# Regrouping the routing of a mixture-of-experts layer: groups of 3, 4, 4, 4 and 1 batches

## The chip, the cores and the metric

The kernel runs on one core of a Trainium2 chip. The metric is the device time of one execution in microseconds, as the median of several runs. The engines are named as in the profile: PE multiplies matrices, PEld is its weight load, DVE, ACT and POOL are the vector, scalar and general engines, and SP issues most DMAs.

## The reference

Two decoder layers with layer norms ahead of each part: self-attention, cross-attention over a context of 375 rows and a mixture of experts, twice. There are 16 batches of 112 tokens, 256 wide. The change concerns the seam between the second layer's cross-attention and its mixture of experts. The router of that mixture is this, cut to what matters:

```python
logits = x @ router_w + router_b                     # 8 experts
top, ei = top_k(logits, 2); probs = softmax(top)
# per batch: first choices of all tokens, then second choices, are counted up per expert
pos = cumsum(one_hot(ei), axis=0) * one_hot - 1       # place of the token in its expert's buffer
# 33 places per expert and batch; tokens past these are dropped
buf[ei, pos] += x
h = buf @ w_c_fc + b_c_fc;  g = buf @ w_gate + b_gate
o = silu(h * g) @ w_c_proj + b_c_proj
out = x + sum_k probs[k] * o[ei[k], pos[k]]
```

## The kernel before

The work is tiled by batch: the 112 tokens of one batch lie on partitions. The second cross-attention is one loop over 32 steps `(b, u)`, batch and half of the heads. A step turns the softmaxed scores of this step on PE (L1493), issues the scores of the next one (L1461, row maxima L1472, Exp L1473, division on POOL L1484), takes one item from a list called `after`, and then makes keys and values of the next batch, the projection of the batch before (L1315 adds it to `x_res`), the queries, and the values (L1509). The keys and values of batches 4, 8 and 12 (and 0) were made earlier in the program and are loaded, so the steps of batches 3, 7 and 11 have less PE work; batch 15 has no successor.

PE's order in this section is the order of the program (`manual_schedule` for PE). DVE, ACT, POOL and SP are put in order by the compiler's scheduler, and each then runs its list strictly in that order. In the section that follows, the feed-forward part, DVE and PE both follow the program.

The list `after` carries the routing. `routed(b)` makes a batch's logits (`logits1`, L1219 adds the bias). With the fourth batch of a group, `route1` finds the two best experts of the four batches on the DVE (`top_two`, L297 to L305) and makes the two softmax shares (`prob`, L1227 to L1231). It returns `places`, which takes the counting products with a triangle of ones on PE (here called P) and from these, on the DVE, each token's position, expert, slot number `place`, and the number `need` of tokens per expert past the first 12 (L1247 to L1264). After it come four `dispatch1`: `slot_rows` builds a 0/1 row of 264 slots for each token (L1285, L1286) and normalises x again (L238), PE multiplies the two (L1275, the slot products), and DVE (first half) and ACT (second half) copy the result into `first_in` and `more_in` (L1278, L1279). The last group, batches 12 to 15, is not in the list: it is routed and dispatched at the head of the feed-forward section.

There, `ranks` orders the experts by `need` (L1660 to L1681) and gives the numbers by which weights for the fullest experts are fetched; SP waits for them ahead of the third weight unit. Then come 12 units: two experts by number and one by rank, four times. `hidden(n, j)` makes one of eight products of a unit, with ACT (L1766) and DVE (L1767) behind it, and each `hidden` is followed by one item of the list `jobs` (bias rows by rank, and the matrices of softmax shares by which results are added up).

Some names more: `mv1` and `r1` are mean and reciprocal deviation of each token (POOL makes the latter, L242 and L243), `xn15` is the normalised batch 15, kept in its own place because the last projection writes it there.

Of the kernel before, what the change touches and what calls it, by code (L numbers as in the profile page):

```python
# [9 lines left out]
F32 = mybir.dt.float32  # L10
U32 = mybir.dt.uint32
AF = mybir.ActivationFunctionType
# [17 lines left out]
P0 = 12  # L30
# [8 lines left out]
def _constants():  # L39
# [31 lines left out]
        "slots": rows(np.arange(E1 * CAP)),  # L71
# [27 lines left out]
def tile_decoder(ctx: ExitStack, tc: tile.TileContext, t: dict, out: bass.AP):  # L99
# [137 lines left out]
    def normed(dst, src, mv, r):  # L237
        nc.vector.tensor_scalar(dst, src, mv, r, ALU.subtract, ALU.mult)  # L238
# [6 lines left out]
    def norm_one(lp, b, keep=None, affine=None, dst=None):  # L245
# [10 lines left out]
        normed(xn, x[:, b, :], mv[:, 0:1], r)  # L256
# [30 lines left out]
    def top_two(lp, v, n, rev):  # L287

        nb = v.shape[1]
        bn = lambda name: lp.tile([L, nb, n], F32, tag=f"tt_{name}", name=name, bufs=1)  # L290
        b1 = lambda name: lp.tile([L, nb], F32, tag=f"tt_{name}", name=name, bufs=1)
# [929 lines left out]
    def route1(lp, q):  # L1221

        bs = slice(4 * q, 4 * q + 4)
        (oh0, v0), (oh1, v1) = top_two(lp, lg1[:, bs, :], E1, const("rev8", L))

        p0, ex = prob[0][:, bs], prob[1][:, bs]
        nc.vector.tensor_sub(ex, v1, v0)  # L1227
        nc.scalar.activation(ex, ex, AF.Exp)
        nc.vector.tensor_scalar(p0, ex, 1.0, None, ALU.add)
        nc.vector.reciprocal(p0, p0)  # L1230
        nc.vector.tensor_mul(ex, ex, p0)  # L1231

        oh = [o.rearrange("p b n -> p (b n)") for o in (oh0, oh1)]

        def places():
            pc = bank()
            before = const("before", L)
            mm_sum(pc[:L, : 4 * E1], [(before, oh[0])])
            mm_sum(pc[:L, 4 * E1 : 8 * E1], [(before, oh[1]), (ones[:L, :L], oh[0])])
            b1 = lambda name: lp.tile([L, 4], F32, tag=f"rt_{name}", name=name, bufs=1)  # L1240
            tmp = lp.tile([L, 4, E1], F32, tag="rt_tmp", name="tmp", bufs=1)
            sums = lp.tile([L, E1], F32, tag="rt_sums", name="sums", bufs=1)
            for k in range(2):
                pos, ok, more = b1(f"pos{k}"), b1(f"ok{k}"), b1(f"more{k}")
                o3 = (oh0, oh1)[k]
                kept, ei = pos1[k][:, bs], exp1[k][:, bs]
                nc.vector.tensor_tensor(  # L1247
                    tmp, o3, pc[:L, 4 * k * E1 : 4 * (k + 1) * E1].rearrange("p (b n) -> p b n", n=E1), ALU.mult
                )
                nc.vector.tensor_reduce(pos, tmp, AX.X, ALU.add)  # L1250
                nc.vector.tensor_tensor(tmp, o3, over(const("io8", L), 4), ALU.mult)
                nc.vector.tensor_reduce(ei, tmp, AX.X, ALU.add)
                nc.vector.tensor_scalar(ok, pos, CAP - 0.5, None, ALU.is_lt)

                nc.vector.tensor_scalar(kept, pos, float(CAP - 1), None, ALU.min)

                nc.vector.scalar_tensor_tensor(pos, ei, float(CAP), kept, ALU.mult, ALU.add)
                nc.vector.scalar_tensor_tensor(pos, pos, 1.0, ok, ALU.add, ALU.mult)
                nc.vector.tensor_scalar(place[k][:, bs], pos, -1.0, None, ALU.add)

                nc.vector.tensor_scalar(more, kept, P0 - 0.5, None, ALU.is_gt)
                nc.vector.tensor_tensor(tmp, o3, bcast(more, E1), ALU.mult)
                nc.vector.tensor_reduce(sums, tmp.rearrange("p b n -> p n b"), AX.X, ALU.add)
                nc.vector.tensor_add(need, need, sums)  # L1264

        return places

    def dispatch1(lp, b, made=None):
# [4 lines left out]
        for c in range(2):  # L1273
# [3 lines left out]
            copy = nc.scalar.copy if c else nc.vector.tensor_copy  # L1277
# [3 lines left out]
    def slot_rows(lp, b):  # L1281
        slots = const("slots", L)
# [4 lines left out]
        xn = lp.tile([L, D], F32, tag="xn", name="xn", bufs=2)  # L1287
        normed(xn, x[:, b, :], mv1[:, b, 0:1], r1[:, b : b + 1])
# [8 lines left out]
    with ExitStack() as ph:  # L1297
# [243 lines left out]
        with tc.manual_schedule(engines={mybir.EngineType.PE}):  # L1541
# [46 lines left out]
            after = []  # L1588

            def routed(b):  # L1590
                logits1(b)
                if b % 4 == 3:
                    q = b // 4
                    places = route1(rp, q)
                    after.append(places)
                    if q < B // 4 - 1:
                        after.extend(lambda b=b: dispatch1(lp, b) for b in range(4 * q, 4 * q + 4))
# [38 lines left out]
        after.append(lambda: routed(B - 1))  # L1636
        while len(after) > 1:
            after.pop(0)()
# [7 lines left out]
    with ExitStack() as ph:  # L1646
# [180 lines left out]
        with tc.manual_schedule(engines={mybir.EngineType.DVE, mybir.EngineType.PE}):  # L1827
            late.pop(0)()
            while after:
                after.pop(0)()  # L1830
            made = {b: slot_rows(lp, b) for b in (B - 4, B - 3)}
            ranked = ranks()
            for b in range(B - 4, B):
                dispatch1(lp, b, made.pop(b))
                if b + 2 < B:
                    made[b + 2] = slot_rows(lp, b + 2)
            jobs = bias_of(0)
            jobs += share_jobs(share_first, KA, first_idx)
# [69 lines left out]
```

## Time and profile before

| | |
|---|---|
| Runs (us) | 1610.70, 1608.06, 1604.71 |
| Median (us) | 1608.06 |
| Profiled execution (us) | 1611.35 |
| Its span (us) | 1609.6 |
| Mean granted PE clock | 0.973 |
| DMA moved | 116.52 MB |

The profile is of one execution. Times within it count from the start of its span. The cross-attention loop of the second layer runs from about 954 to 1316 us, the feed-forward section from then to the end. "Idle before, releaser" beside an instruction is how long its engine stood and what ended it. The loop is told by its step number n = 2b + u; the step begins with its transposes (L1493).

### The profile page before, as it was taken

The page shows a single profiled execution, that of the slowest core. Times are in us where ns is not written, and L with a number is a line of the kernel's source. Part 1 is how long each engine was busy: PE and PEld are TensorE (multiplying, and loading weights), DVE is VectorE, ACT ScalarE, POOL GpSimd, SP SyncE. Part 2 cuts the span into 40 slices and gives each one's busy share as a digit, 9 for nine tenths or more (in the row PEclk, how much of TensorE's full clock was granted, in tenths as well). Part 3 has the DMA queues.
Part 4 walks back from the last instruction along what each step waited for, and adds up shares of the span by engine and source line. Part 5 has one row for each costly group of instructions (what it writes and reads, how often), then busy time and mean ns, then how long its engine had stood idle before and what let it go on. Part 6 is the DMA issues. An engine that isn't in the chain of part 4 may idle for free.

```text
span 1609.6 us, 30346 instructions
## 1 busy us (share of the span) xinstructions
PE 1501.8 (93%) x11438; PEld 1127.5 (70%) x11438; DVE 964.1 (60%) x2649; ACT 577.9 (36%) x1437; POOL 483.1 (30%) x647
## 2 busy tenths in 40 slices
PE   7898999999988896899999989999999978999998
PEld 5776777777754585778888756666666657788786
DVE  6986777777762353976677655566575566342124
ACT  3441444444442252223333233343434323333332
POOL 5642122222115352323333344544445420000000
PEclk9999999999999897999999999999999988999999
DMA  6500322222224476200000010101010012344421
GB/s 170 143 10 21 94 67 65 67 65 65 64 76 158 130 231 214 54 24 1 1 1 2 20 56 10 49 20 48 19 30 30 1 53 79 137 178 157 147 89 48
DMA packets 84929, 116.52 MB, mean 72 GB/s; under 512 B 13433, under 2 KB 70946, under 8 KB 84778
## 3 DMA queue, kind: packets, MB, share of 16 engines
q1 hardware_dynamic: 78690, 98.25, 20.1%
q0 software_dynamic: 3312, 8.54, 1.6%
q10 hardware_dynamic: 2776, 7.72, 1.4%
q8 instruction: 95, 1.56, 0.4%
q14 instruction: 56, 0.46, 0.1%
HBM read 84.41 MB, written 22.08 MB: 66 GB/s over the span
## 4 chain that ended last, share of the span: by engine, by line
PE 76%; DVE 13%; POOL 4%; DMA 3%; issue 2%; another core or an unknown queue 1%; ACT 1%; SPq 0%; POOLq 0%; DVEq 0%; ACTq 0%
PE pT L120 49%; PE pT L785 3%; PE pT L1461 3%; PE pT L1493 2%; POOL pr L1484 2%; DVE mx L769 2%; PE pT L1509 2%; PE pT L803 2%; PE pT L767 2%; PE pT L1358 2%; PE pT L1393 2%; PE pT L1379 2%; PE pT L620 1%; DVE st L234 1%
## 5 line engine op out<-in xcount | busy, mean ns | idle before, releaser
L1484 POOL TENSOR_SCALAR pr<-pr,den 112x375 f32<-112x375 f32 x128 | 157.0, 1244 | 176.9 <-DVE den L1482 157.7
L120 PE MATMUL pT<-xnT,w_all 128*128 128x224 f32 (+2 forms) x800 | 165.3, 358 | 0.6 <-DVE xnT L269 0.5
L120 PEld LDWEIGHTS pT<-xnT,w_all 128*128 128x128 f32 x800 | 145.9, 197 | 10.2 <-issue 5.7
L794 ACT ACTIVATE pr<-pT 125x336 f32<-125x336 f32 x256 | 94.6, 456 | 126.3 <-PE pT L785 126.3
L769 DVE TENSOR_REDUCE mx<-pT 112x1 f32<-112x375 f32 x256 | 122.2, 539 | 11.3 <-PE pT L767 9.9
L1371 POOL TENSOR_TENSOR pr<-pr,den 112x448 f32<-112x448 f32 x64 | 59.9, 956 | 198.8 <-DVE den L1369 147.9
L120 PE MATMUL pT<-w_all 128*128 (+3 forms) x376 | 113.1, 453 | 1.7 <-ACT w_all L392 0.8
L120 PE MATMUL pT<-w_all,cT 128*125 128x256 f32 (+1 forms) x336 | 111.4, 475 | 0.0
L120 PE MATMUL pT<-cT,w_all 128*128 128x375 f32 x320 | 110.2, 486 | 0.0
L120 PE MATMUL pT<-w_all,xnT 128*112 128x256 f32 (+1 forms) x320 | 105.7, 477 | 1.9 <-ACT xnT L566 0.9
L120 PE MATMUL pT<-w_all,oT 128*112 128x256 f32 x448 | 106.4, 383 | 0.6 <-DVE oT L1400 0.6
L242 POOL TENSOR_SCALAR nr<-nmv 112x1 f32<-112x1 f32 x96 | 22.3, 232 | 273.7 <-DVE nmv L235 273.1
L1308 ACT COPY pT<-pT 112x448 f32<-112x448 f32 (+1 forms) x64 | 34.0, 532 | 170.9 <-PE pT L1493 88.3
L120 PEld LDWEIGHTS pT<-w_all 128*128 128x128 f32 (+2 forms) x376 | 70.2, 190 | 33.8 <-issue 4.6
L1473 ACT ACTIVATE pr<-pT,top 112x375 f32<-112x375 f32 x128 | 72.4, 572 | 56.8 <-DVE top L1472 54.4
L120 PEld LDWEIGHTS pT<-cT,w_all 128*128 128x128 f32 x320 | 59.3, 190 | 41.1 <-issue 5.8
L120 PEld LDWEIGHTS pT<-w_all,oT 128*112 128x112 f32 x448 | 75.7, 177 | 16.3 <-DVE oT L1400 1.0
L120 PE MATMUL pT<-first_in,w_all 128*128 128x192 f32 x512 | 86.6, 329 | 0.0
L120 PEld LDWEIGHTS pT<-first_in,w_all 128*128 128x128 f32 x512 | 84.4, 192 | 1.5 <-issue 0.3
L120 PEld LDWEIGHTS pT<-w_all,cT 128*125 128x125 f32 x336 | 61.1, 187 | 33.3 <-issue 22.7
L120 PEld LDWEIGHTS pT<-w_all,xnT 128*112 128x112 f32 x320 | 57.1, 183 | 35.8 <-issue 22.4
L1767 DVE SCALAR_TENSOR_TENSOR hT<-pT,vT,gt 128x192 f32<-128x192 f32 x64 | 26.7, 417 | 90.5 <-ACT gt L1766 90.4
(306 smaller groups left out, 3019.2 us busy)
## 6 DMA issues: line engine op xcount, KB each, us to landing
w_all<-in_L_ffn_w_c_fc_dram SPq DMA_DIRECT2D x12, 1024.0 KB
w_all<-in_L_ffn_w_gate_dram SPq DMA_DIRECT2D x12, 1024.0 KB
w_all<-in_L_ffn_w_c_proj_dram SPq DMA_DIRECT2D x12, 1024.0 KB
cx<-in_ctx_dram SPq DMA_DIRECT2D x32, 375.0 KB
kz<-kn SPq DMA_DIRECT2D x128, 46.9 KB
xg<-w_all SPq DMA_DIRECT2D x1, 5547.0 KB
xb<-xg SPq DMA_DIRECT2D x36, 129.0 KB
yb<-yo SPq DMA_DIRECT2D x16, 224.0 KB
```

The lines of the kernel that those rows point to most:

```text
L120: mm(o, l, r, start=(i == 0), stop=(i == len(terms) - 1))
L767: mm(ps[i][:L, :S], qz[b % 2][r, g, :], kz[b % 2][r, g, :], start=True, stop=True)
L769: nc.vector.tensor_reduce(mx[b % 2][:, g, i, 16:17], ps[i][:L, :S], AX.X, ALU.max, negate=True)
L785: mm(pw[i][:KC, j * L : (j + 1) * L], kz[b % 2][r, g, j * KC : (j + 1) * KC], qm[r, :], start=True, stop=True,)
L794: nc.scalar.activation(pr[:, i, :], pw[i][:KC, : NKC * L], AF.Exp)
L803: mm(po[32 * i : 32 * i + 32, :L], va[b % 2][:, j, 4 * g + i, :], pr[:, i, j * L : (j + 1) * L], start=(j == 0), stop=(j == NKC - 1),)
L1308: nc.scalar.copy(dst, src)
L1358: mm(ps[k][:L, s * L : (s + 1) * L], q, kk, start=True, stop=True)
L1371: nc.gpsimd.tensor_tensor(pr[:, k], pr[:, k], bcast(den[:, k, :], L), ALU.mult)
L1461: mm(ps[2 * s + k][:L, :S], qTs[b // 2][rows(k), m, (b % 2) * L : (b % 2 + 1) * L], kTs[b][rows(k), m, :], start=True, stop=True,)
L1473: nc.scalar.activation(pr[:, i, :], ps[i][:L, :S], AF.Exp, bias=top[:, i : i + 1], scale=1.0, accum_out=den[:, i : i + 1],)
L1484: nc.gpsimd.tensor_scalar(pr[:, n, :], pr[:, n, :], den[:, n : n + 1], None, ALU.mult)
```

## The change

Batches are grouped as 0 to 2, 3 to 6, 7 to 10, 11 to 14, and 15 alone. `route1` takes a first batch and a count, and returns two functions: `places` with all that the slot numbers need, and `counts` with softmax and `need`. For the first four groups both run together as one item of `after`, and their slot products follow in the list, but for batches 13 and 14. These two and batch 15 are dispatched in the feed-forward section: the normalised rows of 13 and 14 are made on POOL, right behind the normalisation of batch 15, and their products are copied out by ACT alone; batch 15 uses `xn15`. The counts of batch 15 and then `ranks` become items of `jobs`, so they run behind the first products of the feed-forward part. In `places`, the slot number is one larger and the slots table starts one later, which saves a subtraction, and the clipped position `kept` is made on POOL.

```diff
     def route1(lp, b0, nb):
...
-                nc.vector.tensor_scalar(kept, pos, float(CAP - 1), None, ALU.min)
-                nc.vector.scalar_tensor_tensor(pos, ei, float(CAP), kept, ALU.mult, ALU.add)
-                nc.vector.scalar_tensor_tensor(pos, pos, 1.0, ok, ALU.add, ALU.mult)
-                nc.vector.tensor_scalar(place[k][:, bs], pos, -1.0, None, ALU.add)
+                to = place[k][:, bs]
+                nc.vector.scalar_tensor_tensor(to, ei, float(CAP), pos, ALU.mult, ALU.add)
+                nc.vector.scalar_tensor_tensor(to, to, 1.0, ok, ALU.add, ALU.mult)
+                nc.gpsimd.tensor_scalar(kept, pos, float(CAP - 1), None, ALU.min)
+        def counts():
+            p0, ex = prob[0][:, bs], prob[1][:, bs]
...
+            for k in range(2):
+                more = b1(f"more{k}")
+                nc.vector.tensor_scalar(more, pos1[k][:, bs], P0 - 0.5, None, ALU.is_gt)
...
+            ENDS = (2, 6, 10, 14, 15)
             def routed(b):
                 logits1(b)
+                if b in ENDS:
...
+                    places, counts = route1(rp, b0, b + 1 - b0)
+                    if b < B - 1:
+                        after.append(lambda: (places(), counts()))
+                        after.extend(lambda b=b: dispatch1(lp, b) for b in range(b0, b + 1))
+                    else:
+                        after.extend((places, counts))
...
-        after.append(lambda: routed(B - 1))
-        while len(after) > 1:
+        while B - 2 not in done or len(after) > 2:
             after.pop(0)()
...
+            two = {}
+            for b in (B - 3, B - 2):
+                two[b] = lp.tile([L, D], F32, tag="xn", name="xn", bufs=2)
+                with tc.issue_after(normed_last[0].ins):
+                    nc.gpsimd.tensor_scalar(
+                        two[b], x[:, b, :], mv1[:, b, 0:1], r1[:, b : b + 1], ALU.subtract, ALU.mult
+                    )
+            made = {b: slot_rows(lp, b, two[b]) for b in (B - 3, B - 2)}
             late.pop(0)()
-            while after:
-                after.pop(0)()
-            made = {b: slot_rows(lp, b) for b in (B - 4, B - 3)}
-            ranked = ranks()
-            for b in range(B - 4, B):
-                dispatch1(lp, b, made.pop(b))
-                if b + 2 < B:
-                    made[b + 2] = slot_rows(lp, b + 2)
-            jobs = bias_of(0)
-            jobs += share_jobs(share_first, KA, first_idx)
+            routed(B - 1)
+            _, _, places, counts = after
+            dispatch1(lp, B - 3, made[B - 3], (nc.scalar.copy,) * 2)
+            places()
+            dispatch1(lp, B - 2, made[B - 2], (nc.scalar.copy,) * 2)
+            dispatch1(lp, B - 1, slot_rows(lp, B - 1, xn15))
+            ranked = []
+            jobs = [counts] + share_jobs(share_first, KA, first_idx)
+            jobs.insert(4, lambda: ranked.extend(ranks()))
+            jobs[5:5] = bias_of(0)
```

## The prediction

> **What bounds the kernel now.** I read the page first, then the tail of the second cross-attention by stretches, then PE's waits and its timeline there, then the DVE's timeline. The page:
>
> ```profile
> span 1609.6 us, 30346 instructions
> PE 1501.8 (93%) x11438; PEld 1127.5 (70%) x11438; DVE 964.1 (60%) x2649; ACT 577.9 (36%) x1437; POOL 483.1 (30%) x647
> PE 76%; DVE 13%; POOL 4%; DMA 3%; issue 2%; another core or an unknown queue 1%; ACT 1%; SPq 0%; POOLq 0%; DVEq 0%; ACTq 0%
> ```
>
> PE is the bound almost everywhere; an edit pays where PE waits, and costs where it adds work to PE. By stretches (time, then busy us of PE, PE's loads, DVE, ACT, POOL, then granted clock, DMA share and GB/s):
>
> ```profile
> 1307.40:1316.70 9.30, 6.39 (x39) 5.18 (x40) 6.24 (x19) 0.61 (x2) 0.26 (x1) 0.63 0.01 3
> 1316.70:1325.20 8.50, 6.02 (x27) 4.70 (x25) 4.38 (x15) 1.81 (x6) 0.80 (x2) 0.76 0.42 123
> 1325.20:1333.50 8.30, 1.51 (x6) 1.27 (x6) 6.83 (x43) 0.20 (x1) 0.00 (x0) 0.50 0.00 0
> 1333.50:1342.70 9.20, 6.90 (x18) 4.75 (x19) 8.12 (x31) 1.81 (x6) 0.00 (x0) 0.69 0.00 1
> 1342.70:1355.60 12.90, 12.90 (x73) 12.62 (x73) 6.71 (x24) 6.59 (x14) 0.00 (x0) 0.91 0.05 6
> ```
>
> The last projection ends at 1316.7, the first feed-forward product starts at 1342.7: 26.0 us in which the DVE, routing four batches at once, sets the pace and PE runs at half clock for much of it. In the last stretch PE is full again. Now PE's waits over 960 to 1345, and the pieces around them:
>
> ```profile
> PE pT L1493 <- POOL pr L1484: 8.0, 13, 0.8
> PE pT L1275 <- DVE xn L238: 6.5, 4, 2.9
> PE pT L1660 <- DVE need L1264: 4.8, 1, 4.8
> ...
> 1119.15 1.16 PE L1275 MATMUL pT<-dm,xn 112*128 112x264 f32 x4
> 1127.73 1.20 PE L1275 MATMUL pT<-dm,xn 112*128 112x264 f32 x4
> 1134.55 0.58 PE L1493 MATMUL pT<-call,pr 112*125 112x112 f32 x3 [0.63 <-POOL pr L1484]
> 1310.31 2.10 PE L1275 MATMUL pT<-dm,xn 112*128 112x264 f32 x4 [2.94 <-DVE xn L238]
> 1328.89 0.19 DVE L1247 TENSOR_TENSOR tmp<-oh,pT 112x32 f32<-112x32 f32 x1
> 1342.73 13.05 PE L120 MATMUL pT<-first_in,w_all 128*128 128x192 f32 x72
> ```
>
> In the attention loop the only waits are for POOL's softmax scaling, in the short steps beside batches 4, 8 and 12, whose keys were made ahead. Elsewhere in the loop PE never waits, so a piece put there costs its full length.
>
> **The change part by part.** I number the 32 loop steps n = 2b + u and follow the list `after`, from which each step takes one item. Pieces of PE by the timeline: logits of one batch about 0.4 us, rank products of a group (P) about 0.6, slot products of one batch about 0.95 (neighbours' starts 0.9 to 1.0 apart).
>
> *Loop.* Before, the steps 4 to 31 take 13 logits, 3 P and 9 slot products; after, 12 logits, 3 P and 11 slot products. The steps that matter are 14, 15, 22, 23, next to waits for POOL. Before they hold slot products 2, 3, 5 and 6, after only logits 4, 5, 7 and 8. Outside these and 30, 31, before has 13 x 0.37 + 2 x 0.57 + 4 x 0.95 = 9.7 us and after 7 x 0.37 + 3 x 0.57 + 10 x 0.95 = 13.8: +4.1 us of PE work where PE is full. The short steps give back little, since POOL's end does not move: step 14 stood 0.16 us behind POOL's end anyway, and step 15 gains about the 0.4 us of a normalisation (L238) that the DVE no longer runs ahead of the row maxima. Two pairs give back 1.0. **Loop: +3.1.**
>
> *Last step.* After the transposes (end 1307.4) PE waits 2.94 us for the slot rows of batch 8, which stand behind group 8 to 11's ranks on the DVE. Their place is taken by the logits of batch 11, ready long before. Then the chain is logits 0.4, transposes of batch 14 (its xn ends at 1308.1), values about 2.1 cold, projection 1.9: end at 1312.7 instead of 1316.7. **-4.0.** If the cover goes, because xn 14 comes later, the wait returns in part (0 to 2 us).
>
> *Tail, from the projection's end Tp.* Before: 26.0. After, on the DVE in its order: logits 12 to 14 follow the projection on PE, so top two starts at Tp+1.7; 11 dependent steps took 2.44 (1325.41 to 1327.85), with the normalisation of batch 15 between: Tp+4.6. P and its wait took 1.04 (to 1328.89): 5.6. Softmax (four DVE steps, an Exp) fits into that wait. Places are 14 steps instead of 26 (4.6 us before); by the first half's own spacing 2.8: 8.4. Slot rows of 11 and 12, 0.35 + 0.49 each: 10.1. The eight counting steps, 1.7, and two first-half evictions of 0.75: 13.3. Slot rows of 13, 14, 1.7: 15.0. Then batch 15: xnT copy to logits 1.6, top two 2.2, P 1.0, places 2.5, slot rows 0.85, PE and eviction 1.4: 24.6. I take 25.1 for waits between. The four evictions of 13 and 14, moved to ACT (0.32 and 0.47 each), end while the DVE ranks batch 15; ACT was busy 3.8 of 26.0 us here. The wider slots table (one step of 0.17 less for each choice) and the kept normalisation of batch 15 (0.41 less) are in these counts. ranks (11 DVE steps, 2.1 us) and softmax and counts of batch 15 leave the path. What keeps the gain small is that the first group of four is still routed here, with its own top two, P and places, and a fifth chain follows. **-0.9.**
>
> The granted clock in this stretch bears on three PE pieces of the path (logits, P, slot products). The row says 0.50 from 1325.2 to 1333.5. The Trainium skill, "TensorE: Matmul & The Clock Gate", section "Part 1: The HAM clock gate", puts the clock at half after about 3.4 us of idling and at full after a sustained window. Cold, these pieces cost 0.9, 1.0 and 0.9; at full clock half, and Tp+23.3. PE is even less busy here than before, so I keep the cold prices.
>
> *Feed-forward.* In the first unit the DVE gets counts (12 steps and an Exp round trip, 2.9) and ranks (2.1) beside what it had: jobs and eight products 12 us in a unit of 12.9. The last product ends some 2 us later than before relative to the start; its consumer stood 1.3 us off. **+0.7.** The Exp bears on a rule against this change: "ScalarE: Activation LUTs", section "What ACT_TABLE_LOAD costs", has every switch of function set cost about 2.66 us with its drain. The trace shows one such load, 1.28 us at 1347.15, for the first Silu. The job stands ahead of that Silu, so 0 is taken; if ACT's order puts the Exp behind it, two more loads come, 2.6 by the row or 5.3 by the page, of which PE's lead of three products (four us) hides most: 0 to +2. By SP's waits, its wait for the ranks before unit 2's weights lasted 20.0 us before and then the buffer was not free until 1353.9; the ranks now come about then, and behind them lie 8 to 10 us before the weights are used: 0.
>
> *POOL.* Two normalisations of 256 columns each: by L1484 (1.235 us for 375) about 0.85 each, from Tp+3, needed by Tp+17: 0. "GPSIMD Engine Reference", section "4.1 Engine selection", warns of POOL for elementwise work; here ten us cover it. `kept` (two tiny steps a group) is new on POOL, and the counts wait for it. The nearest row is L242, 0.22 us. Behind a scaling queue of 4.87 it is 0 to 4.9 each; I take 0, since the DVE stands still up to 3.6 us for POOL in the loop now without PE waiting. Its low end is a gain of the four DVE steps saved, nil on a full PE.
>
> Sum: +3.1 - 4.0 - 0.9 + 0.7 = -1.1. The profiled execution took 1611.35 (span 1609.6 and 1.75 around it), 3.3 above the median of the runs; the same difference on the median gives 1607.0.
>
> **The rivals.** *Full gain.* The moved slot products find room after all, because PE's starts hide a few tenths per step, and the compiler's order of the DVE interleaves the two routings: loop 0, tail 21.8 (the DVE's pure busy time, no wait). -4.0 - 4.2 + 0.7 = -7.5: 1600.6. For it: the DVE is 60% busy. Against: the loop's steps differ by just the piece they take, 10.95 with logits (n = 25) and 11.5 with slot products (n = 13).
>
> *Slower: `kept` behind the scaling.* POOL runs strictly in order; if the compiler places `kept` behind a step's four scalings (4.87 us), the DVE stands at `more` with the next row maxima and evictions behind it, and PE waits for these. It decides where that stand exceeds about 3.6 us, the longest that the loop bears now. Two such stands in each of three groups, with 1.5 us each through to PE: +9, so 1616.5. Against it: counts are last in their group, and the compiler may fill ahead of them.
>
> *No change.* The tail only shifts: Tp earlier by what the loop takes, DVE bound as before: 1608.
>
> **How the numbers follow.** A difference under about 0.5% (8 us: 1600.0 to 1616.1) can hardly be told from no change, as the runs of one kernel spread over 6 us. Forecast 0.56, its own range 1602 to 1612; no change 0.13; full gain 0.16, of which about half pass 1600; slower 0.15, mostly past 1616, plus small shares of the others where half-clock windows fall badly (each up to 1.7 us, several in a run). Faster 0.11, same 0.72, slower 0.17. The range that leaves out two in ten reaches 1599 to 1618.
>
> **What would show it.** Right: no 2.94 us wait before the slot products at the last step; projection's end near 1316 and first feed-forward product near 1341; loop steps 10 to 13 and 18 to 21 longer by about 0.5 each; DVE busy over 21 of the 25 us in between. Wrong: PE waits for DVE or POOL at the steps that take P (9, 17, 26); more than one table load behind the boundary; a gap over 1 us in PE between the first and second unit; or a boundary under 22 us.

## The result, and the profile after

| | before | after |
|---|---|---|
| Median of 13 runs each (us) | 1606.89 | 1612.31 |
| Lowest to highest (us) | 1601.53 to 1610.70 | 1608.05 to 1614.34 |
| Ratio after / before, 95% interval | | 1.0028 [1.0017, 1.0039] |
| Profiled execution, its span (us) | 1611.35, 1609.6 | 1610.24, 1608.5 |

The change costs 0.28%, 4.5 us by the ratio (the medians lie 5.4 apart): small, but its interval lies wholly above 1. The two profiled spans do not show it, because the code ahead of the attention loop, which is the same in both, took 6.5 us less in the profiled execution of after (step 1 begins at 961.47 instead of 967.97). Over the profiles of this study that start moved by up to 17 us (955.71 to 972.68) without an edit ahead of it, so spans are not compared here; stretches counted from step 1 are.

| Stretch (us) | before | after | difference | predicted |
|---|---|---|---|---|
| Step 1 to step 31 | 335.93 | 345.64 | +9.7 | +3.1 |
| Step 31 to the end of its transposes | 3.47 | 3.07 | -0.4 | |
| from there to the end of the last projection | 9.36 | 6.54 | -2.8 | -4.0 |
| from there to the first feed-forward product | 25.99 | 24.42 | -1.6 | -0.9 |
| from there to the end | 266.85 | 267.33 | +0.5 | +0.7 |
| Sum | 641.60 | 647.00 | +5.4 | -1.1 |

So all but one of the stretches came out within 1.2 us of their terms, and the loop did not. The page of after, the span and the engines' busy time:

```profile
span 1608.5 us, 30395 instructions
PE 1508.0 (94%) x11444; PEld 1131.7 (70%) x11444; DVE 963.9 (60%) x2663; ACT 579.3 (36%) x1442; POOL 488.2 (30%) x659
```

PE has six more products than before but is busy for 6.2 us more: nearly the same work, longer. POOL has 12 more instructions.

**The tail** by stretches (time, then busy us of PE, PE's loads, DVE, ACT, POOL, then granted clock, DMA share and GB/s), and from PE's waits over 950 to 1345 those for the DVE:

```profile
1316.60:1322.30 5.70, 2.61 (x19) 2.39 (x17) 3.99 (x22) 0.21 (x1) 0.80 (x2) 0.71 0.55 184
1322.30:1331.90 9.60, 4.10 (x11) 2.90 (x10) 7.50 (x35) 1.20 (x4) 2.80 (x4) 0.64 0.00 1
1331.90:1341.10 9.20, 7.40 (x22) 5.35 (x23) 5.45 (x31) 2.40 (x8) 0.74 (x3) 0.54 0.00 0
```
```profile
PE pT L1284 <- DVE dm L1295: 4.4, 2, 3.2
PE pT L120 <- DVE oh L303: 3.4, 3, 2.4
PE pT L120 <- DVE xnT L271: 2.5, 1, 2.5
```

Before, the long waits were four for normalised rows (6.5 us, of which 2.94 lie in the last step) and one for `need` (4.8). The wait for `need` is gone, as it should be. In its place stands one wait for each link of two chains, one behind the other: best experts (2.4), slot rows (3.2), then batch 15's transposed x (2.5), its best experts (0.33) and its slot rows (1.21). PE's timeline shows this order:

```profile
1310.99 0.38 PE L269 MATMUL pT<-call,xn 112*128 112x112 f32 x2 [0.50 <-DVE xn L238]
1311.82 2.23 PE L1519 MATMUL pT<-pT,vt 125*64 125x112 f32 x24 [0.45 <-DVE pT L1320]
1313.97 2.75 PE L120 MATMUL pT<-w_all,oT 128*112 128x256 f32 x8
...
1320.20 0.55 PE L120 MATMUL pT<-oh,call 112*112 112x32 f32 x2 [2.39 <-DVE oh L303]
1325.64 3.80 PE L1284 MATMUL pT<-dm,xn 112*128 112x264 f32 x8 [3.23 <-DVE dm L1295]
1332.15 0.56 PE L120 MATMUL pT<-router_w,xnT 128*112 128x8 f32 x4 [2.52 <-DVE xnT L271]
1339.25 2.10 PE L1284 MATMUL pT<-dm,w_all 112*128 112x264 f32 x4 [1.21 <-DVE dm L1295]
1341.14 7.59 PE L120 MATMUL pT<-first_in,w_all 128*128 128x192 f32 x40
```

The first three lines belong to the last step: the wait of 2.94 us before batch 8's slot products is gone, and two short ones (0.50 and 0.45) have come. The third is the last projection.

**The loop.** Its 9.7 us fall into three parts, found by comparing each step with the same step of before and of the first experiment below (the change with `kept` on the DVE):

- *More work in full steps, +3.1.* Steps 9 to 11, 17 to 20, 26 to 30 are longer by 0.2 to 0.6 each; steps 13, 14 and 22 are shorter by 0.5, and 21 by 0.3. Without steps 8, 16 and 24, which vary with the clock, these differences add up to 3.03 in the version with `kept` on the DVE.
- *POOL, +2.4.* Steps 10, 18 and 27 take 14.27, 14.34 and 13.63 instead of 13.41, 13.41 and 13.01 with `kept` on the DVE. These are the steps behind the ones that take P.
- *Half clock, +4.2.* Step 24 takes 18.73 instead of 14.54. This is the part that varies most between executions: experiments 6 and 11 below have the loop of experiment 1 and spent 15.63 and 15.67 in this step, and 340.10 and 340.25 us in the whole loop instead of 344.98.

How `kept` costs time can be read in the timeline of step 9 and 10. `kept` is the POOL instruction of 0.24 us; the second fence is PE's own timeline, the third the same place in experiment 1, where PE does not wait:

```profile
1054.91 2.46 POOL L1494 TENSOR_SCALAR pr<-pr,den 112x375 f32<-112x375 f32 x2 [6.92 <-DVE den L1492]
1055.49 0.17 DVE L1245 TENSOR_REDUCE pos<-tmp 112x3 f32<-112x24 f32 x1
1057.45 0.24 POOL L1254 TENSOR_SCALAR pos<-pos 112x3 f32<-112x3 f32 x1
1057.68 2.50 POOL L1494 TENSOR_SCALAR pr<-pr,den 112x375 f32<-112x375 f32 x2
1057.73 0.17 DVE L1270 TENSOR_SCALAR more<-pos 112x3 f32<-112x3 f32 x1 [1.50 <-POOL pos L1254]
1060.42 0.17 DVE L1270 TENSOR_SCALAR more<-pos 112x3 f32<-112x3 f32 x1 [0.88 <-POOL pos L1254]
...
1066.01 0.57 ACT L1483 ACTIVATE pr<-pT,top 112x375 f32<-112x375 f32 x1 [2.84 <-DVE top L1482]
```
```profile
1066.73 1.98 PE L120 MATMUL pT<-w_all,oT 128*112 128x256 f32 x8 [0.31 <-ACT pr L1483]
```
```profile
1066.17 1.89 PE L120 MATMUL pT<-w_all,oT 128*112 128x256 f32 x8
```

The input of `kept` was there at 1055.66; it ran at 1057.45, when POOL had finished the two softmax scalings that stood ahead, and the `kept` of the second choice had two more ahead of it. The DVE stood at `more` for 1.50 and 0.88 us, with evictions and row maxima behind it in its order; ACT then stood 2.84 us for row maxima, and PE 0.31 for ACT. All in all the DVE stood at `more` for 8.4 us:

```profile
DVE more L1270 <- POOL pos L1254: 8.4, 6, 1.9
```

And step 24, PE's timeline around 1224. First after, then before at the same place:

```profile
1220.25 0.58 PE L1503 MATMUL pT<-call,pr 112*125 112x112 f32 x3 [0.44 <-POOL pr L1494]
1221.46 0.58 PE L1503 MATMUL pT<-call,pr 112*125 112x112 f32 x3 [0.63 <-POOL pr L1494]
1222.67 0.58 PE L1503 MATMUL pT<-call,pr 112*125 112x112 f32 x3 [0.63 <-POOL pr L1494]
1223.88 0.97 PE L1503 MATMUL pT<-call,pr 112*125 112x112 f32 x3 [0.63 <-POOL pr L1494]
1224.78 2.85 PE L1471 MATMUL pT<-kt,qt 64*112 64x375 f32 x8
```
```profile
1224.90 0.58 PE L1493 MATMUL pT<-call,pr 112*125 112x112 f32 x3 [0.63 <-POOL pr L1484]
1226.11 0.58 PE L1493 MATMUL pT<-call,pr 112*125 112x112 f32 x3 [0.63 <-POOL pr L1484]
1227.32 0.58 PE L1493 MATMUL pT<-call,pr 112*125 112x112 f32 x3 [0.63 <-POOL pr L1484]
1227.83 1.52 PE L1461 MATMUL pT<-kt,qt 64*112 64x375 f32 x8
```

The transposes wait for POOL in much the same way. In after the clock went to half at 1223.4 for 10.2 us, and eight score products take 2.85 instead of 1.52 us; before, it stayed full. Ahead of this, the emptied step 23 has logits (0.56) where before had slot products (1.20).

### The profile page after: what moved, and what is told of

Its sections match the earlier page's. It is cut to its first block, busy times and chain, and to the rows that moved or that the text cites. A ratio compares the mean times of both kernels' runs of the same rounds, so it can differ in the third digit from the quotient of the medians.

```text
span 1608.5 us, 30395 instructions
## 1 busy us (share of the span) xinstructions
PE 1508.0 (94%) x11444; PEld 1131.7 (70%) x11444; DVE 963.9 (60%) x2663; ACT 579.3 (36%) x1442; POOL 488.2 (30%) x659
## 4 chain that ended last, share of the span: by engine, by line
PE 76%; DVE 13%; POOL 5%; DMA 3%; issue 2%; ACT 1%; SPq 0%; POOLq 0%; ACTq 0%; DVEq 0%
PE pT L120 49%; POOL pr L1494 3%; PE pT L787 3%; PE pT L1471 2%; PE pT L1503 2%; DVE mx L771 2%; PE pT L805 2%; PE pT L1519 2%; PE pT L769 2%; PE pT L1368 2%; PE pT L1389 2%; PE pT L1403 2%; PE pT L622 1%; DVE st L234 1%; PE pT L1823 1%
## 5 line engine op out<-in xcount | busy, mean ns | idle before, releaser
L120 PE MATMUL pT<-w_all,oT 128*112 128x256 f32 x448 | 109.8, 392 | 1.2 <-ACT pr L1483 0.6
L120 PE MATMUL pT<-hT,w_all 128*128 128x192 f32 (+1 forms) x384 | 79.7, 366 | 0.0
```

The costliest lines, as they stand in the source:

```text
L120: mm(o, l, r, start=(i == 0), stop=(i == len(terms) - 1))
```

## The experiments

All ratios are to the kernel before, run beside the experiments on the same chip, with 95% intervals. Beside experiments 1 to 8 it took 1606.4, beside 9 to 11 it took 1615.16: there the ratios can be set beside the others, the times cannot.

**1. `kept` back on the DVE.**

```diff
-                nc.gpsimd.tensor_scalar(kept, pos, float(CAP - 1), None, ALU.min)
+                nc.vector.tensor_scalar(kept, pos, float(CAP - 1), None, ALU.min)
```

> The changed kernel with one edit: the clipped position is made on the DVE again instead of on POOL. Theory A (the loop grew because slot products moved from the short steps, where POOL sets the pace, into steps that PE fills): the DVE does two steps more a group and PE's order is as in the changed kernel, so the ratio to before stays near 1.0028, within 1 us. Theory B (the DVE stands behind POOL's scaling at the counting step, 8.4 us in six stands in the changed profile, so row maxima come late and PE waits in steps 10, 18 and 27): those stands vanish, steps 10, 18 and 27 get 0.8, 0.8 and 0.6 us shorter, about 2 us in all, ratio near 1.0015. Theory C (half-clock windows after the emptied short steps, 10.2 us of them in step 24 of the changed profile against none before) expects no change from this edit.

Measured: 1608.93, 1.0009 [0.9997, 1.0021]. The 0.86, 0.93 and 0.62 us of steps 10, 18 and 27 are gone, and PE's waits for ACT with them. `kept` on POOL is worth about 0.19%, 3 us. The intervals of the two ratios overlap; the three steps of the profile, and experiment 7 below, are what shows the cost. The loop of this profile still took 344.98, because step 16 fell into half clock as well as step 24 (17.34 and 18.73).

**2. Groups of 4, 4, 4, 3 and 1,** all else as in the change.

```diff
-            ENDS = (2, 6, 10, 14, 15)
+            ENDS = (3, 7, 11, 14, 15)
```

> The changed kernel with groups of 4, 4, 4, 3 and 1 instead of 3, 4, 4, 4 and 1. The loop's list is then item for item that of before (slot products in steps 14, 15, 22, 23 and 31), while the head of the feed-forward part stays as in the changed kernel but for the logits of batch 12, which are ready in the loop. Theory A: the loop from step 1 to step 31 takes 336 us as before instead of 345.6 (or 341 without the half-clock windows), the 2.9 us wait ahead of batch 8's slot products comes back, and three slot products more lie behind the projection (2 to 4 us): ratio between 0.997 and 1.001. Theory B: the stands at the counting step stay, so steps 12 and 21, which follow a group's rank products, are 0.8 us longer each than before: 1.5 us of the loss stays. Theory C: no half-clock window of 10 us at step 24.

Measured: 1616.50, 1.0053 [1.0036, 1.0071]. The work of the loop's steps is that of before again, but step 21 grew from 11.88 to 14.29, the last step's wait is back (12.07 us from transposes to the projection's end), and the tail is 26.49. This was slower than the 0.997 to 1.001 expected. It has a fifth chain in the tail and nothing gained for it: experiment 7 below, also with `kept` on POOL but with one chain in the tail, has 1.0006.

**3. Slot products into the short steps.** The change, but each step picks its item by kind (d slot products, r logits, p the counting products P): the short ones slot products first, the others logits first.

```diff
...
-                    after.pop(0)()
+                    order = "drp" if b % 4 == 3 else "rpd"
+                    ok = [i for i, f in enumerate(after) if f.kind != "d" or "p" not in [g.kind for g in after[:i]]]
+                    after.pop(min(ok, key=lambda i: (order.index(after[i].kind), i)))()
...
```

> The changed kernel, same groups and same work, but each loop step chooses from the list: the short steps (batches 3, 7, 11, 15) take a slot product if one is ready, the others take logits first. Steps 14, 15, 22, 23, 30, 31 then hold slot products 2, logits 5, slot products 5, 6, 8, 9; the changed kernel has only slot product 10 there. Theory A: four slot products leave full steps for short ones against logits, 4 x 0.55 = 2.2 us less on PE, less 0.5 given back at each short pair: 1 to 2 us under the changed kernel, and the wait ahead of step 31's slot product costs up to 3 again; ratio 1.001 to 1.004. Theory C: with PE busier in steps 14, 15, 22 and 23 the half-clock windows at steps 16 and 24 shrink to those of before (3.4 us or none): 2 to 4 us less. Theory B expects no change.

Measured: 1611.02, 1.0028 [1.0017, 1.0039], the same as the change. The loop fell from 345.64 to 341.30, but the last step and the tail took 8.06 and 25.56 instead of 6.54 and 24.42, in a profile whose half clock in the tail lasted 23.9 us against 20.4. No gain from filling alone can be told.

**4. Behind alone.** The kernel before, with its groups of four and everything else; only softmax, counts and ranks of the last group are moved behind the slot products.

```diff
...
-            while after:
-                after.pop(0)()
+            after.pop(0)()
+            after.pop(0)()
...
-            ranked = ranks()
+            ranked = []
...
-            jobs = bias_of(0)
-            jobs += share_jobs(share_first, KA, first_idx)
+            jobs = [after.pop(0)] + share_jobs(share_first, KA, first_idx)
+            jobs.insert(4, lambda: ranked.extend(ranks()))
+            jobs[5:5] = bias_of(0)
```

> The kernel before with one part of the change alone: softmax and counts of the last group of four and the ranks become items behind the first feed-forward products; groups of 4, POOL and copies as before. Theory A: the loop stays as before, and the stretch from the last projection to the first feed-forward product loses the ranks (2.1 us of DVE), the eight counting steps (1.7) and what of softmax was not hidden (0.7): 21.5 to 23 us instead of 26.0, of which 0.5 to 1 comes back in the first unit: ratio near 0.998, faster than both. If the stretch is not bound by the DVE's count of steps, 1.000.

Measured: 1599.46, 0.9951 [0.9934, 0.9968], in five runs: more than twice the gain expected, which was a ratio of 0.998. The loop is that of before (335.84), and the tail is 19.82 instead of 25.99, below the 21.5 to 23 expected. Its stretches from the counting products on, and PE's timeline there:

```profile
1323.20:1328.80 5.60, 0.95 (x4) 0.82 (x4) 4.09 (x23) 0.00 (x0) 0.00 (x0) 0.50 0.00 0
1328.80:1334.75 5.95, 5.90 (x16) 4.32 (x16) 5.13 (x17) 1.83 (x6) 0.00 (x0) 0.64 0.00 0
1334.75:1347.75 13.00, 13.00 (x81) 12.85 (x81) 9.46 (x47) 7.43 (x17) 0.00 (x0) 1.00 0.03 5
```
```profile
1323.45 0.95 PE L120 MATMUL pT<-oh,call 112*112 112x32 f32 x4 [0.70 <-DVE oh L301]
1328.85 5.94 PE L1278 MATMUL pT<-dm,xn 112*128 112x264 f32 x16 [4.45 <-issue]
1334.75 6.89 PE L120 MATMUL pT<-first_in,w_all 128*128 128x192 f32 x40
```

There is one chain of the DVE, one long wait (4.45, for which the profile names no releaser; the DVE is at work for 4.09 us of its stretch), and then all slot products of four batches run back to back, 16 matmuls in 5.94 us, straight into the feed-forward part, which runs at full clock (1.00). The tail before was 6.2 us longer, with softmax, counts and ranks in between; there the same 16 products took from 1334.75 to the first feed-forward product at 1342.73, with two waits among them.

**5. The rest of the change with groups of four,** `kept` on the DVE: behind, the shortened slot number, batch 15's kept normalisation, two normalisations on POOL.

```diff
-            ENDS = (2, 6, 10, 14, 15)
+            ENDS = (3, 7, 11, 15)
...
-            for b in (B - 3, B - 2):
+            for b in (B - 4, B - 3):
...
```

> The changed kernel with groups of four as before, the clipped position on the DVE, and all else kept: softmax, counts and ranks behind, the shorter places, batch 15 from its stored normalisation, and the two first normalised rows (of batches 12 and 13) on POOL. Theory D (regrouping alone is the loss: it adds 3 us to the loop, and its fifth chain of top two, products and places takes back 4.6 us at the head of the feed-forward part): the loop is that of before, 336 to 338, the stretch from projection to first product at most the 19.8 us of softmax, counts and ranks behind alone, less up to 1.5 for the steps saved: ratio 0.993 to 0.996, the fastest so far. Rival (the regrouping was needed to hide the rest, and what failed is the place of the clipped position alone): ratio near 1.000.

Measured: 1601.72, 0.9977 [0.9967, 0.9988]. Faster than before, but less so than the 0.993 to 0.996 expected. Against experiment 1, which has the same parts in the new groups, the loop is 335.92 instead of 344.98 and the tail 20.71 instead of 24.42: the regrouping costs 0.32% here, and the intervals of the two do not overlap.

**6. Regrouping alone.** Experiment 1 with counts and ranks put back ahead of the last slot products; its other parts stay.

```diff
             places()
+            counts()
+            ranked = ranks()
...
-            ranked = []
-            jobs = [counts] + share_jobs(share_first, KA, first_idx)
-            jobs.insert(4, lambda: ranked.extend(ranks()))
-            jobs[5:5] = bias_of(0)
+            jobs = bias_of(0)
+            jobs += share_jobs(share_first, KA, first_idx)
```

> The changed kernel with the clipped position on the DVE and with counts, softmax and ranks of batch 15 put back ahead of its slot products: groups of 3, 4, 4, 4 and 1, but nothing behind the first products. Theory D: the two parts add up, regrouping +8 us and putting behind -7, so this one loses what putting counts and ranks of one batch behind had hidden, about 4 us (12 counting and softmax steps, 11 of ranks): ratio near 1.0035 to 1.005, and the stretch from projection to first product near 28 us. Rival (with one batch in the last group those steps hide beside the products of batch 14 and 15 anyway): as without the edit, 1.001.

Measured: 1616.72, 1.0072 [1.0044, 1.0100], in six runs from 1603.36 to 1621.00. The profile is of the fastest of them. Its tail is 29.72, and the wait for the ranks is back beside the second chain:

```profile
1328.11 0.59 PE L1676 MATMUL pT<-need,call 112*128 112x8 f32 x2 [4.61 <-DVE need L1273]
```

**7. Behind, with `kept` on POOL, in groups of four.** Experiment 4 with the slot number made from the unclipped position.

```diff
...
-                nc.vector.tensor_scalar(kept, pos, float(CAP - 1), None, ALU.min)
...
+                to = place[k][:, bs]
+                nc.vector.scalar_tensor_tensor(to, ei, float(CAP), pos, ALU.mult, ALU.add)
...
+                nc.gpsimd.tensor_scalar(kept, pos, float(CAP - 1), None, ALU.min)
...
```

> Softmax, counts and ranks behind with groups of four, as measured at 0.9951, and one edit: the clipped position is made on POOL, and the slot number from the unclipped one, with as many DVE steps less one a choice. Theory B: the DVE stands at the counting step behind POOL's scaling; steps 12, 21 and 31 or those around them, where slot rows follow the counts, get longer, 2 to 5 us in all: ratio 0.9965 to 0.998. Rival (the stands were an effect of the regrouped order): 0.995.

Measured: 1607.37, 1.0006 [0.9993, 1.0020] against 0.9951 and 0.9964 (experiments 4 and 9): one tiny instruction per choice takes back all that "behind" gives, 7 to 9 us. The DVE stood at `more` for 9.8 us in six stands. From the timeline of steps 20 and 21:

```profile
1184.05 0.22 POOL L1252 TENSOR_SCALAR pos<-pos 112x4 f32<-112x4 f32 x1
1184.31 0.17 DVE L1265 TENSOR_SCALAR more<-pos 112x4 f32<-112x4 f32 x1 [1.90 <-POOL pos L1252]
1187.57 0.17 DVE L1265 TENSOR_SCALAR more<-pos 112x4 f32<-112x4 f32 x1 [1.70 <-POOL pos L1252]
1192.98 1.57 PE L1465 MATMUL pT<-kt,qt 64*112 64x375 f32 x2 [1.45 <-DVE vt L1451]
1195.16 0.57 ACT L1477 ACTIVATE pr<-pT,top 112x375 f32<-112x375 f32 x1 [4.88 <-DVE top L1476]
```

Two stands of 1.90 and 1.70 us become 1.45 us of PE for an eviction and 4.88 of ACT for row maxima; a half clock of 6.8 us began at 1193.0, and step 21 took 17.15 us instead of 11.49. In experiment 2, which also has `kept` on POOL and the same groups there, it took 14.29 without a half clock.

**8. Short steps padded.** Experiment 1, with the logits of batches 4, 5, 7 and 8 issued three times: useless work for PE where the change has emptied the steps.

```diff
-        mm_sum(pl[:L, :E1], ...)
+        for _ in range(3 if b in (4, 5, 7, 8) else 1):
+            mm_sum(pl[:L, :E1], ...)
```

> The changed kernel with the clipped position on the DVE (1.0009), and with the logits products of batches 4, 5, 7 and 8, which stand in the short steps 14, 15, 22 and 23, issued three times instead of once: 0.66 us more of PE work in each, with the same result. Theory C (half-clock windows at steps 16 and 24 come from PE's low load in the emptied short steps): the extra work lies in PE's waits, so it costs 0 to 1 us by itself, and the half-clock time at steps 16 and 24 falls from 17 us to 10 or less: ratio at or under 1.000. If the load there does not decide: half-clock time as before, ratio 1.001 to 1.0025.

Measured: 1606.67, 1.0000 [0.9983, 1.0016] against 1.0009 [0.9997, 1.0021]: useless work made nothing slower, and perhaps something faster, but the intervals overlap. In its profile step 24 took 13.77 (18.73 without padding), while step 16 took 16.82 (17.34). That fits an account by half clock, but it doesn't settle it: without padding, experiments 6 and 11 took 15.63 and 15.66 in step 16, less than the padded kernel, and 15.63 and 15.67 in step 24.

**9. Behind alone, once more,** the same kernel as in experiment 4.

> The kernel before with softmax, counts and ranks of its last group of four moved behind the slot products, once more, beside the next two. If the -7 us (0.9951) of its five runs is the edit's own, 0.993 to 0.997 again; if those runs were only lucky in where the half clock fell, 0.998 to 1.000.

Measured: 1608.60 where the kernel before took 1615.16, 0.9964 [0.9951, 0.9978], in 11 runs. So the gain of experiment 4 was not luck of its five runs.

**10. Behind, with the shortened slot number and batch 15's kept normalisation,** experiment 5 without POOL.

```diff
...
-            made = {b: slot_rows(lp, b, two[b]) for b in (B - 4, B - 3)}
+            made = {b: slot_rows(lp, b) for b in (B - 4, B - 3)}
```

> Groups of four as before, behind as in the kernel of the row above, and all other parts of the change that need no regrouping: the place without clip and -1 step, the kept normalisation of batch 15; nothing of it on POOL. Fewer DVE steps in the tail (4 of 0.17 and one of 0.41, about 1.1 us) on a stretch that the DVE bounds: if the other parts are worth their steps, 1 us faster than the kernel of the row above, 0.9945; if PE's half-clock windows set the tail, the same as it, 0.995; if the normalisations on POOL were a help in the fours version of the change (0.9977), slower than 0.998.

Measured: 1609.46, 0.9970 [0.9957, 0.9982]: the same as experiment 9. About five DVE steps fewer bring nothing that can be told; the tail of this profile was 22.51, with 17.1 us of half clock against 10.2 in experiment 9's.

**11. The normalisations of batches 13 and 14 back on the DVE,** on top of experiment 1.

```diff
...
-            made = {b: slot_rows(lp, b, two[b]) for b in (B - 3, B - 2)}
+            made = {b: slot_rows(lp, b) for b in (B - 3, B - 2)}
```

> The changed kernel with kept on the DVE and the normalisations of batches 13 and 14 on the DVE too, in the slot rows, as those of the other batches. They ended at 1332.2 on POOL, after a wait, while the DVE needed them at about 1329. If POOL's part there is a cost: first FFN product 1 us earlier, 1.0003. If it is free: the DVE gets 0.8 us more work in its chain, 1.0014.

Measured: 1616.67, 1.0018 [1.0005, 1.0030] against 1.0009 [0.9997, 1.0021], not told apart. The profiles say why there is nothing to tell. First the change, where POOL normalises beside the DVE's slot rows, then this experiment, where the DVE does it all (its two normalisations are lines like the L238 one):

```profile
1329.48 0.36 DVE L1294 TENSOR_SCALAR d<-call,place 112x264 f32<-112x264 f32 x1 [0.18 <-PE pT L1284]
1329.62 2.57 POOL L1849 TENSOR_SCALAR xn<-x_res,mv,r 112x256 f32<-112x256 f32 x2 [5.26 <-PE pT L1284]
1329.87 0.67 DVE L1295 SCALAR_TENSOR_TENSOR dm<-call,place,d 112x264 f32<-112x264 f32 x1
1330.58 0.52 DVE L1294 TENSOR_SCALAR d<-call,place 112x264 f32<-112x264 f32 x1
1331.14 0.66 DVE L1295 SCALAR_TENSOR_TENSOR dm<-call,place,d 112x264 f32<-112x264 f32 x1
1331.72 0.38 DVE L271 COPY xnT<-pT 128x224 f32<-128x224 f32 x1
```
```profile
1336.30 0.36 DVE L1294 TENSOR_SCALAR d<-call,place 112x264 f32<-112x264 f32 x1 [0.28 <-PE pT L1284]
1336.69 0.49 DVE L1295 SCALAR_TENSOR_TENSOR dm<-call,place,d 112x264 f32<-112x264 f32 x1
1337.10 0.41 DVE L238 TENSOR_SCALAR xn<-x_res,mv,r 112x256 f32<-112x256 f32 x1
1337.42 0.35 DVE L1294 TENSOR_SCALAR d<-call,place 112x264 f32<-112x264 f32 x1
...
1338.54 0.38 DVE L271 COPY xnT<-pT 128x224 f32<-128x224 f32 x1
```

From the first slot row to the copy of batch 15, both take 2.24 us. The DVE does two steps of 0.41 less, and its other steps get as much longer while POOL runs beside them (`dm` 0.67 and 0.66 instead of 0.49, the second `d` 0.52 instead of 0.35).

**Read together,** the experiments make a table of two groupings by two places of `kept`, all with "behind":

| | `kept` on DVE | `kept` on POOL |
|---|---|---|
| groups of four | 0.9951, 0.9964 | 1.0006 |
| 3, 4, 4, 4, 1 | 1.0009 | 1.0028 (the change) |

and without "behind", `kept` on the DVE: 1 (before) and 1.0072 (regrouped). The lower row and the 1.0072 have the other parts of the change too (the shorter slot number, batch 15's kept normalisation, two normalisations on POOL), the upper row has not; with them, and `kept` on the DVE, groups of four have 0.9977 (experiment 5). So "behind" gives 0.4 to 0.6% in either grouping, the regrouping takes 0.3% (experiment 5 against 1, the closest pair) to 0.7%, and `kept` on POOL takes 0.2% with the new groups and 0.4 to 0.55% with the old ones. The change is about their sum. The best version is experiment 4 and 9, some 0.7% faster than the change; experiments 5 and 10 cannot be told from 9.

## Why the prediction was wrong

The prediction was -1.1 us; measured were +4.5 by the ratio and +5.4 by the stretches of the profile. By its own steps:

**Loop, +3.1: right for what it counted, and short of what came on top.** The slot products that move from the short steps into full ones cost 3.03, step by step. Its sign of being right, steps 10 to 13 and 18 to 21 longer by 0.5 each, held only in part: 12 was unchanged, 13 and 21 were shorter, and 9, 17 and 26 to 30 grew as well. The other 6.6 us of this profile are two terms that the sum held at nothing.

**`kept` on POOL, "0 to 4.9 each; I take 0": this step failed.** It cost 2.4 us in the loop's profile and 0.19% (3 us) by the ratios of the change and experiment 1; with `kept` on the DVE, 1.4 us of loss are left (-0.5 to +3.4). The reason given, that the DVE stands up to 3.6 us for POOL in the loop now without PE waiting, does not carry over: it compared the length of one stand with that of another. The stands were shorter than the tolerated ones, 1.9 us at the longest. In the steps where PE was late, evictions and row maxima were queued behind the waiting instruction. The rival named this mechanism and put it at +9, from a stand of 3.6 us on; the threshold was wrong and the price was too high for this grouping. With groups of four it is about right (7 to 9 us between experiments 4 or 9 and 7, much of it in step 21). The sign to look for was one step off: PE was late not in the steps that take P (9, 17, 26) but in those behind them (10, 18, 27).

**The clock had no place in the loop's term.** The prediction allowed for half-clock windows in its chances, up to 1.7 us each, but its sum weighed the clock in the tail alone. Over its 13 runs the mean granted clock was 0.9708 after; the kernel before had 0.9722 over the 43 runs beside experiments 1 to 4. Within one kernel a run with 0.001 less took about 0.7 to 1.6 us more. By that slope the clock goes with an estimated 1 to 2 us of the 4.5; the slope does not say what brought the clock down, so this is not a cause beside the others. The 4.2 us of step 24 are that of one execution: step 24 took 14.5 to 16.2 us in all kernels with groups of four, and in the regrouped ones 13.8 (padded), 15.6, 15.7, 17.3, and 18.7 twice. That emptied short steps bring on these windows is one reading. That only their place in time decides, which differs between executions of the same loop, is another. No experiment here tells them apart.

**Last step, -4.0: mis-sized, -2.8 in this profile.** The wait of 2.94 us went, as forecast. But behind it the transposes of batch 14 waited 0.50 us for its xn and the values 0.45 for an eviction, where the sum had "0 to 2 us if the cover goes" and took none of it; and the last projection took 2.75 instead of 1.9, with half clock up to 1315.6. Other profiles with the same last step had 5.10 (experiment 6) to 7.63 (experiment 11) instead of 6.54, so -4.0 lies within what single executions do.

**Tail, -0.9: right within its size, -1.6.** The chain went as laid out: batch 15's transposed x, its best experts, places and slot rows follow the first chain, and 24.42 came again within 0.02 us in experiments 1, 8 and 11. The DVE was busy for 16.95 us of the 24.42, though, where the forecast had over 21 of 25: waits between the engines filled more of it than laid out. The normalisations on POOL, taken as 0.85 us each and nothing on the path, took 1.28 each, started at 1329.6 rather than three microseconds after the projection (POOL stood 5.26 us for slot products), and cost the DVE what they saved (experiment 11). The price of 1.7 for the slot rows of 13 and 14 was 2.2. The cold prices were right for most of it: the granted clock was 0.71, 0.64 and 0.54 in its three stretches, and 24.4 lies between the 25.1 taken and the 23.3 for full clock.

**Feed-forward, +0.7: right, +0.5.** In after there is one table load, at 1346.67, as before; the job stands ahead of the first Silu.

**Luck.** The forecast had the projection's end near 1316 and the first feed-forward product near 1341, and the profile has 1316.72 and 1341.14. These agree because this execution reached the loop 6.5 us earlier; counted from step 1, both came later than before by 6.5 and 4.9 us. Three sums of the prediction do not come out of its own figures, without bearing on its result: the slower rival's +9 on 1607.0 is 1616.0, not 1616.5; halving the three cold pieces once each gives 23.7, not 23.3; and 21.8 us is not the DVE's busy time in the tail, which was 19.33 before.

**What the prediction did not ask.** It summed the change as a whole. Taken apart, "behind" is worth 6 to 8 us, and it found this neither in the forecast nor in the rival of full gain, which reached -7.5 by assuming that the loop's cost and the waits of the two chains vanish. Its own sentence, "a fifth chain follows", held the answer: experiment 1's tail is 24.4; with one chain of four it is 20.7 in experiment 5, which has the same other parts, and 19.5 to 19.8 without these. The regrouping was to spare the last step's wait (-2.9 between experiments 5 and 1) and paid for it 3.4 in the loop (steps 8, 16 and 24 aside) and 3.7 in the tail, and some more in half clock and in the feed-forward section (267.0 to 267.9 us in the regrouped kernels, 265.3 to 266.9 in those with groups of four).

## What to carry to other kernels

Price the parts of a change one by one, with each other part absent: here one part was worth 6 to 8 us of gain and two others took back more, and the sum looked like nothing much. A tiny instruction moved to an engine that works in long pieces can cost what is queued behind the one that waits for it, not its own 0.24 us; ask what the waiting engine has to do next and for whom. In a tail that hangs on one engine's chain, moving work out of that chain paid here (6.2 us), while splitting the chain in two brought back a wait at every link.

## What the runs showed of the hardware

- Half clock came without a long wait. At the start of step 24 of the changed kernel PE stood 0.44, 0.63, 0.63 and 0.63 us between transposes from 1219.8 on, with no longer wait in the ten microseconds ahead, and the clock was at half for 10.2 us from 1223.4. Such waits are not enough by themselves: before had three of 0.63 us at the same place and stayed at full clock. Which of the loop's places are hit differs between executions even where the program is the same: step 8 took 15.6 to 15.7 us in twelve of the thirteen profiles and 18.83 in that of experiment 9, whose kernel is that of experiment 4 (15.67). "TensorE: Matmul & The Clock Gate", section "Part 1: The HAM clock gate" of the Trainium skill, names an idle window of about 3.4 us and says that the window is free-running; the lengths in the loop and the tail (3.4, 6.8, 10.2, 13.7, 17.1, 23.9, 27.3) are multiples of it, but no wait of that length stood ahead of the half clock in step 24.
- POOL took 1.28 us for a normalisation of 112 x 256 that takes the DVE 0.41, and DVE steps of two SBUF inputs beside it were 0.17 to 0.18 us longer. The Trainium skill, "GPSIMD Engine Reference", section "8. Key points", names contention with DVE instructions "in a 2-port perf mode or with two SBUF inputs"; in this case the longer steps made the offloading worth nothing, 2.24 us either way. A `d` step, with one large input, was longer too (0.52 instead of 0.35); which of the two cases it falls under, if any, no run here shows.
